# A four-stage macaron network on one core: the conditional tiles of the routed FFN moved ahead of the main experts, its table and zero writes moved to other places

## The chip, the cores and the metric

The kernel runs on one NeuronCore of a Trainium2 chip. The metric is the device time of one execution in microseconds (us). Before the change its median over 8 runs is 1976.63 us, from 1973.01 to 1981.93.

The core has five engines with instruction queues of their own, which meet through semaphores: PE (TensorE: matmuls; its weight loads are listed as PEld), DVE (VectorE), ACT (ScalarE), POOL (GpSimd) and SP (SyncE, which here only issues transfers). SP, ACT and POOL can each start DMA transfers from their queue. In the profile a name with a q behind it (PEq, POOLq, SPq) is the engine's sequencer: branches, semaphore steps and DMA issues.

## The reference

The activations are x of [2, 512, 256] in fp32: T = 1024 tokens of D = 256. Ten stages with residual additions follow each other: an FFN, an attention and an FFN of layer 0, one stage of layer 1, FFN, attention, FFN of layer 2, FFN, attention, FFN of layer 3 (the FFNs of one layer share their weights; each FFN's result is added with a factor 0.5). The FFNs of layers 0 and 3 are routed, and they are what the change touches. In the text they are FFN1 and FFN2 (layer 0), FFN3 and FFN4 (layer 3), in the order of time. Layer 0's reads:

```python
scores = softmax(x2d @ wg_router.T)                 # 32 experts
topk_w, topk_idx = top_k(scores, 6)
topk_w = topk_w / (sum(topk_w) + 1e-20)
C = 2 * (T * 6 // 32)                               # capacity of an expert: 384 slots
pos_in_e = position of the token in its expert's list
valid = pos_in_e < C                                # what does not fit is dropped
g = einsum('ecd,edf->ecf', xe, w_gate);  u = einsum('ecd,edf->ecf', xe, w_up)
ye = einsum('ecf,efd->ecd', silu(g) * u, w_down)    # F = 176
y = sum over the 6 of  y_tok * topk_w
out = y + silu(x2d @ ws_gate) * (x2d @ ws_up) @ ws_down   # shared expert, 352 wide
```

Layer 3's has 8 experts, 2 of them for a token, sigmoid scores, a factor 2.5, no capacity below T, and a shared expert of 176. The norm ahead of each FFN is a layer norm without weights.

## The kernel before, in words

`moe()` (L638) is called four times, by `l0_ffn` and `l3_ffn`. The 1024 tokens lie as 128 partitions by 8 chunks (P = 128, NC = 8), in two halves of four chunks (B = 2, CB = 4). The text of the program sets the order of instructions on each engine only in part: a scheduler places them, and two means tie it down. `in_order` (L141) chains all instructions of the named engines that are issued inside it, and leaves the last one of each in a dictionary `tail`. `issue_after(i)` keeps what stands inside it behind instruction i.

One routed FFN goes like this:

- Six gather buffers `xes` are cleared by POOL. The pool of weights has five buffers: the shared expert's `wsh` and four experts' `we` fill it, and the fifth expert takes the place of `wsh`.
- Front: per half, four warm-up matmuls, the layer norm (DVE takes moments at L215 and L216; POOL computes the reciprocal deviation `ln_rstd` in two steps, an addition at L224 and a power at L225; DVE writes `xn` at L230), then PE transposes `xn` (L184) into `xT`. The router's logits follow (L326). These are chained on PE and ACT. Behind them, ACT puts the two halves of `xn` into `table` in DRAM (L675), from which tokens are gathered later.
- Where the capacity is below T (FFN1 and FFN2), POOL's queue writes zeros over `rows` in DRAM, eight transfers of 768 KB (L681), so that dropped tokens contribute nothing.
- Scores: in FFN1 and FFN2 a softmax of DVE steps around one exp of ACT (L746 to L751). `topk` (L308 to L318), then `slot_lists` (L424 to L514): DVE builds the one-hot rows `sl_ol` and `sl_oh` (L465, L467, L476), PE multiplies them (`ps_sl`, L484), transposes (`ps_slt`, L504), and DVE writes the index lists `sl_put` and `sl_get` (L513, L514). The normalised scores `lg` go beside the rows in `table` (L692, from ACT's queue).
- The shared expert (`shared_unit`, L364): gate and up products (`pg`, `pu`, L376), silu on ACT (L379), the product `h` on DVE (L380), the down product `acc` on PE (L386), and x <- x + acc on DVE (L404).
- `experts_sparse` (L517) for the main tiles, the first two slot tiles of an expert in layer 0, three in layer 3: it loads an expert's three weights from SP's queue (L530 to L532), POOL gathers a tile of tokens with an indirect DMA (`xe`, L538), PE transposes it (`ps_xe`, L554, DVE copies it to `xeT`), multiplies with gate and up (`ps_gu`, L566), DVE and ACT make `he`, PE transposes it and multiplies with down (`ps_ye`, L591), and POOL scatters the result to `rows` (L596). Before the first tile PE runs eight warm-up passes (L164).
- `prepare_next` (L175) issues what the next stages want early: rows and columns of constants on POOL's queue (among them the bias row of layer 1's FFN, which DVE multiplies by 0.5 at L1113), and loads of layer 2's weights on SP's queue.
- Behind the experts stands a conditional: an integer `over`, computed with the lists, says whether any expert has more tokens than the main tiles hold. All engines load it (L706) and branch (L708); where it is not zero, `experts_sparse` runs once more for the remaining tiles. In the profiled execution the body is not executed: L538 ran 176 times, 128 for layer 0 and 48 for layer 3, which are the main tiles.
- `add_rows` (L714): SP loads a token's result rows back (`y<-rows`, L721) and they are added to x, by DVE (L731, L734) or through PE (`ps_add`, L727).

Of the kernel before, what the change touches and what calls it, by code (L numbers as in the profile page):

```python
# [15 lines left out]
PSUM = bass.MemoryType.PSUM  # L16
DRAM = bass.MemoryType.DRAM

P = 128
B, S, D = 2, 512, 256  # L20
T = B * S
NC = T // P
# [61 lines left out]
class Net:  # L84
# [554 lines left out]
    def moe(self, pre, names, E, F, K, FS, PER, tiles, cap, r, scores, scale):  # L639


        nc, tc, a = self.nc, self.tc, self.a
        router, wg, wu, wd, sg, su, sd = (a[pre + n] for n in names)
        RW = D + E
        self.calls += 1
        with ExitStack() as es:
            lists = es.enter_context(tc.tile_pool(name="f0li", bufs=1))
            table = self.dram.tile([T, RW], F32, name=f"table{self.calls}")
            rows = self.dram.tile([r * T, D], F32, name=f"rows{self.calls}")
            rv = rows.rearrange("(c p n) d -> c p n d", p=P, n=r)  # L650
            xes = [lists.tile([P, 2, RW], F32, name=f"xe{i}") for i in range(6)]
            for t in xes:
                nc.gpsimd.memset(t, 0.0)
            with ExitStack() as fs:
# [6 lines left out]
                with tc.tile_pool(name="ln", bufs=1) as lp:  # L661
                    tv = table[:, :D].rearrange("(b c p) d -> b p c d", p=P, b=B)
                    rT = self.router_weights(sb, psM, router, E)
                    tail, xns = {}, []
                    with self.in_order(tail, ("PE", "Activation")):
                        for b in range(B):
                            self.warm(psM, 4)
                            xn = lp.tile([P, CB, D], F32, name=f"xn{b}")
                            self.layernorm(lp, xn, b, *self.scales(lp, b))
                            xns.append(xn)  # L670
                            for k in range(KD):
                                self.transpose_tokens(xn, xT, psM, b, k)
                        s = self.logits(sb, psM, xT, rT, E, warm=True)
                        for b in range(B):
                            nc.scalar.dma_start(tv[b], xns[b])  # L675
                if cap < T:

                    zero = lists.tile([P, D], F32, name="zero")
                    nc.vector.memset(zero, 0.0)
                    for c in range(NC):  # L680
                        nc.gpsimd.dma_start(rv[c, :, :K, :], zero.unsqueeze(1).to_broadcast([P, K, D]))  # L681
                m = sb.tile([P, NC], F32, name="m")
                scores(s, m)
                mask = self.topk(sb, s, E, K)
# [4 lines left out]
                nc.vector.reciprocal(m, m)  # L689
                nc.vector.tensor_scalar(m, m, scale, None, ALU.mult)  # L690
                nc.vector.tensor_tensor(s, s, m.unsqueeze(2).to_broadcast([P, NC, E]), ALU.mult)
                nc.scalar.dma_start(table[:, D:].rearrange("(c p) e -> p c e", p=P), s)  # L692
                blocks = self.load_shared(sg, su, sd, FS)
                with tc.issue_after(tail["PE"]):
                    for half in range(B):
                        self.shared_unit(work, psA, psM, xT, blocks, half, 0.5)
                over = lists.tile([1, 1], I32, name="over")
                nc.vector.tensor_scalar(over, full[0:1, :], float(len(tiles) * P), None, ALU.is_gt)
            ew = es.enter_context(tc.tile_pool(name="f0e", bufs=1))
            with tc.tile_pool(name="f0p", bufs=1, space=PSUM) as psE:  # L700
                self.puts = []
                args = (table, rows, (get, put), (wg, wu, wd), list(range(E)), F)
                self.experts_sparse(ew, psE, xes, *args, tiles, PER)
            self.prepare_next()
            with tc.tile_pool(name="f0q", bufs=1, space=PSUM) as psE:
                some = nc.values_load(over[0:1, 0:1], min_val=0, max_val=1)  # L706
                wp = es.enter_context(tc.tile_pool(name="f0o", bufs=3))
                with tc.If(some > 0):  # L708
                    rest = list(range(len(tiles), -(-cap // P)))
                    self.experts_sparse(ew, psE, xes, *args, rest, PER, ahead=0, wp=wp)  # L710

        ys = {}

# [1494 lines left out]
```

## Time and profile before

| What | Value |
|---|---|
| Median of 8 runs | 1976.63 us (1973.01 to 1981.93) |
| The profiled execution | 1972.45 us, span 1970.6 us |
| Mean granted TensorE clock in it | 0.955 |
| PE / DVE / POOL / ACT busy | 90% / 58% / 46% / 41% of the span |
| DMA | 226.55 MB, 115 GB/s in the mean |
| first slice of the span (49 us) | PE 6 tenths, DMA 9 tenths, 318 GB/s |
| Queues: SP / POOL / ACT | 170.17 MB / 48.45 MB / 5.72 MB |
| FFN1, FFN2: zeros, 8 transfers | POOL's queue, landing 4.8 / 9.9 / 16.9 us after issue (min / median / max) |
| First expert product (`ps_gu`) in FFN1, 2, 3, 4 | 79.95, 503.25, 1170.17, 1888.43 us |
| First result rows loaded back (`y<-rows`) in FFN1, 2, 3, 4 | 248.75, 671.52, 1238.56, 1955.20 us |

The span is cut into 40 equal slices for the coarse view. In a timeline a line gives start, duration, engine, line of the program, operation, out<-in with shapes and count, and in brackets the idle time of the engine before it and what ended that. A group line gives an operation, how often, the shortest, median and longest duration in ns, and the first and last start in us.

### The profile page before, as it was taken

The numbers are of one execution on the slowest core, as the hardware profiler recorded it, in microseconds if no ns is written. First come the engines' busy times: TensorE is split into PE (matmuls) and PEld (weight loads), VectorE is DVE, ScalarE is ACT, GpSimd is POOL, SyncE is SP. The second block draws the span as 40 slices with busy tenths as digits, with TensorE's granted clock in tenths as the row PEclk, the third lists the DMA queues.
The fourth block names the chain that finished last, engine by engine and source line by source line (L and its number), as shares of the span: only waits on it lengthen the run. The fifth ranks groups of instructions, "written<-read, shape, count | busy, mean of one in ns | idle before, by whom it ended". The sixth has DMA issues, their size and how long they took to land. (4 is left out here: it accounts for less than half of the span.)

```text
span 1970.6 us, 30298 instructions
## 1 busy us (share of the span) xinstructions
PE 1768.1 (90%) x10848; PEld 1267.1 (64%) x10848; DVE 1151.5 (58%) x2771; ACT 804.8 (41%) x1380; POOL 911.4 (46%) x915
## 2 busy tenths in 40 slices
PE   6999859899999878899788999789999899999895
PEld 4677626465777655544465467567777677777674
DVE  4533366317433366655676653588777777777543
ACT  1133223311233124410662012377777687777221
POOL 3377746320777540110133126136657457666363
PEclk8999979899999888999899999899999999999998
DMA  9266450040566520000230023534454444544133
GB/s 318 76 192 187 158 193 12 1 160 27 159 188 187 188 91 1 1 22 0 98 109 23 0 60 96 163 129 128 157 170 150 146 154 152 170 150 141 45 100 98
DMA packets 117445, 226.55 MB, mean 115 GB/s; under 512 B 22382, under 2 KB 68828, under 8 KB 117014
## 3 DMA queue, kind: packets, MB, share of 16 engines
q1 hardware_dynamic: 88134, 170.17, 26.9%
q0 software_dynamic: 20608, 48.45, 7.9%
q10 hardware_dynamic: 8528, 5.72, 0.9%
q8 instruction: 96, 1.57, 0.3%
q14 instruction: 79, 0.65, 0.1%
HBM read 195.59 MB, written 41.81 MB: 120 GB/s over the span
## 5 line engine op out<-in xcount | busy, mean ns | idle before, releaser
L538 POOL DMA_INDIRECT xe<-table,sl_get x176 | 179.9, 1022 | 198.6 <-DVE sl_get L514 146.0
L566 PE MATMUL ps_gu<-we,xeT 128*128 128x352 f32 x704 | 224.6, 460 | 0.0
L596 POOL DMA_INDIRECT rows<-ye,sl_put x176 | 176.9, 1005 | 74.1 <-issue 39.6
L1759 DVE SCALAR_TENSOR_TENSOR xc<-pp,L_attn_cols,xc 128x511 f32<-128x511 f32 (+2 forms) x216 | 161.5, 748 | 30.8 <-ACT xc L1755 25.5
L591 PE MATMUL ps_ye<-we,hT 88*128 88x256 f32 x704 | 168.1, 379 | 2.9 <-ACT ye L132 1.7
L571 DVE SCALAR_TENSOR_TENSOR he<-se,xe,ps_gu 128x176 f32<-128x176 f32 x176 | 70.0, 398 | 167.4 <-ACT se L570 165.9
L566 PEld LDWEIGHTS ps_gu<-we,xeT 128*128 128x128 f32 x704 | 126.3, 190 | 55.4 <-DVE xeT L130 1.3
L591 PEld LDWEIGHTS ps_ye<-we,hT 88*128 88x128 f32 x704 | 133.1, 190 | 36.7 <-ACT ye L132 3.6
L1890 PE MATMUL pz<-xT,wt 128*128 128x128 f32 x1152 | 143.5, 278 | 12.3 <-ACT xt L1839 6.2
L1866 DVE SCALAR_TENSOR_TENSOR lm<-lm,jb,top 128x128 f32<-128x128 f32 x576 | 153.7, 342 | 0.0
L1890 PEld LDWEIGHTS pz<-xT,wt 128*128 128x128 f32 x1152 | 136.3, 193 | 17.7 <-issue 9.2
L1975 PE MATMUL yacc<-wt,y 128*128 128x256 f32 x576 | 143.5, 392 | 2.5 <-POOL y L1945 2.2
L1752 PE MATMUL pp<-xT,wx 128*128 128x512 f32 x288 | 139.3, 607 | 3.6 <-ACT dec L1743 0.9
L570 ACT ACTIVATE se<-ps_gu 128x176 f32<-128x176 f32 x176 | 55.9, 318 | 205.2 <-PE ps_gu L566 205.2
L1945 POOL TENSOR_TENSOR y<-y,sg 128x512 f32<-128x512 f32 x72 | 91.7, 1274 | 100.5 <-DVE y L1944 94.5
L1883 POOL TENSOR_TENSOR ce<-ce,CT 128x1024 f32<-128x1024 f32 x54 | 127.9, 2369 | 0.0
L1552 PE MATMUL ps_y<-w8T,xT 128*128 128x512 f32 x256 | 124.2, 619 | 0.0
L1975 PEld LDWEIGHTS yacc<-wt,y 128*128 128x128 f32 x576 | 104.2, 190 | 25.7 <-issue 10.4
L1918 PE MATMUL py<-lm,xt 128*64 128x128 f32 x1152 | 108.4, 282 | 12.1 <-ACT xc L1755 4.5
L1875 DVE TENSOR_TENSOR lm<-lm,M 128x1024 f32<-128x1024 f32 x72 | 87.2, 1216 | 48.4 <-ACT lm L1871 45.5
L1956 POOL TENSOR_TENSOR sqs<-sqs,sq 128x512 f32<-128x512 f32 x56 | 71.4, 1274 | 92.7 <-ACT sq L1955 92.7
L1906 POOL TENSOR_TENSOR xd<-xt,dec 128x512 f32<-128x512 f32 x54 | 56.3, 1043 | 94.7 <-ACT xt L1839 94.7
(404 smaller groups left out, 3528.5 us busy)
## 6 DMA issues: line engine op xcount, KB each, us to landing
lm<-rows SPq DMA_DIRECT2D x72, 512.0 KB
ce<-rows SPq DMA_DIRECT2D x54, 512.0 KB
rows<-zero POOLq DMA_DIRECT2D x16, 768.0 KB, 9.9
y<-rows SPq DMA_DIRECT2D x16, 768.0 KB
we<-in_L_ffn_w_gate_dram SPq DMA_DIRECT2D x64, 176.0 KB
we<-in_L_ffn_w_up_dram SPq DMA_DIRECT2D x64, 176.0 KB
we<-in_L_ffn_w_down_dram SPq DMA_DIRECT2D x64, 176.0 KB
we<-in_L_ffn_w_dram SPq DMA_DIRECT2D x48, 176.0 KB
```

The costliest lines, as they stand in the source:

```text
L538: nc.gpsimd.indirect_dma_start(xe[:, i, :], None, table, bass.IndirectOffsetOnAxis(get[:, e * per + j : e * per + j + 1], 0), bounds_check ...
L566: nc.tensor.matmul(pg, xeT[:, k, i * P : (i + 1) * P], wgu[:, :, k], start=(k == 0), stop=(k == KD - 1))
L591: nc.tensor.matmul(py[:, i, :], hT[:, q, i * P : (i + 1) * P], wd[:, q, :], start=(q == 0), stop=(q == 1))
L596: put_rows = nc.gpsimd.indirect_dma_start(rows, bass.IndirectOffsetOnAxis(put[:, e * per + j : e * per + j + 1], 0), y[:, i, :], None, bou ...
L1552: nc.tensor.matmul(ps, xT[:, k, :], self.w8T[:, k, 2 * e2 : 2 * e2 + 2, :], start=(k == 0), stop=(k == KD - 1))
L1752: nc.tensor.matmul(pp, wv[:, k, :], xT[:, k, b * S : (b + 1) * S], start=(k == 0), stop=(k == KD - 1))
L1759: nc.vector.scalar_tensor_tensor(out[:, 3 - w :], pp[:, : S - 3 + w], cw[:, m, w : w + 1], out[:, 3 - w :], ALU.mult, ALU.add)
L1866: nc.vector.scalar_tensor_tensor(k["lm"][:, h, :], k["lm"][:, h, :], jb[:, k["c"], n : n + 1], top, ALU.add, ALU.min)
L1883: nc.gpsimd.tensor_tensor(k["ce"], k["ce"], ct, ALU.mult)
L1890: nc.tensor.matmul(pz[:, m, :], u["wz"][:, kk, m * P : (m + 1) * P], xT[:, kk, c * P : (c + 1) * P], start=(kk == 0), stop=(kk == KD - 1),)
L1918: nc.tensor.matmul(py[i * HP : (i + 1) * HP, m, :], w[:, h * HP : (h + 1) * HP], v[:, h, :], start=(m == 0 and n == 0), stop=(n == len(src ...
L1975: nc.tensor.matmul(yacc[cc // 2][:, cc % 2, :], k["y"][:, m, :], u["wo"][:, m, :], start=(u["g"] == 0 and m == 0 and cc % 2 == 0), stop=(u ...
```

## The change

Six things move; what is computed stays, apart from six memsets in the body of the conditional.

1. The shared expert's weights are requested ahead of the norm in the text.
2. Each half of `xn` goes to the table from SP's queue as soon as it is written, not from ACT's queue behind the logits. The normalised scores go to the table from SP's queue as well.
3. POOL's instructions are chained in the front too, and the zero rows stand behind the last of them, the second half's power.
4. The conditional tiles stand ahead of the main experts, so all engines load `over` and branch between the shared expert and the first expert. The body clears the six gather buffers first.
5. The main experts' loads stand behind the put of the second half of `xn`.
6. `prepare_next` stands behind that put and behind POOL's last step of the front.

```diff
                     rT = self.router_weights(sb, psM, router, E)
-                    tail, xns = {}, []
-                    with self.in_order(tail, ("PE", "Activation")):
+                    blocks = self.load_shared(sg, su, sd, FS)
+                    tail = {}
+                    with self.in_order(tail, ("PE", "Activation", "Pool")):
                         for b in range(B):
                             self.warm(psM, 4)
                             xn = lp.tile([P, CB, D], F32, name=f"xn{b}")
                             self.layernorm(lp, xn, b, *self.scales(lp, b))
-                            xns.append(xn)
+                            put_x = nc.sync.dma_start(tv[b], xn)
                             for k in range(KD):
                                 self.transpose_tokens(xn, xT, psM, b, k)
                         s = self.logits(sb, psM, xT, rT, E, warm=True)
-                        for b in range(B):
-                            nc.scalar.dma_start(tv[b], xns[b])
                 if cap < T:

                     zero = lists.tile([P, D], F32, name="zero")
                     nc.vector.memset(zero, 0.0)
-                    for c in range(NC):
-                        nc.gpsimd.dma_start(rv[c, :, :K, :], zero.unsqueeze(1).to_broadcast([P, K, D]))
+                    with tc.issue_after(tail["Pool"]):
+                        for c in range(NC):
+                            nc.gpsimd.dma_start(rv[c, :, :K, :], zero.unsqueeze(1).to_broadcast([P, K, D]))
...
-                nc.scalar.dma_start(table[:, D:].rearrange("(c p) e -> p c e", p=P), s)
-                blocks = self.load_shared(sg, su, sd, FS)
+                nc.sync.dma_start(table[:, D:].rearrange("(c p) e -> p c e", p=P), s)
                 with tc.issue_after(tail["PE"]):
                     for half in range(B):
                         self.shared_unit(work, psA, psM, xT, blocks, half, 0.5)
...
             ew = es.enter_context(tc.tile_pool(name="f0e", bufs=1))
-            with tc.tile_pool(name="f0p", bufs=1, space=PSUM) as psE:
-                self.puts = []
-                args = (table, rows, (get, put), (wg, wu, wd), list(range(E)), F)
-                self.experts_sparse(ew, psE, xes, *args, tiles, PER)
-            self.prepare_next()
-            with tc.tile_pool(name="f0q", bufs=1, space=PSUM) as psE:
+            self.puts = []
+            args = (table, rows, (get, put), (wg, wu, wd), list(range(E)), F)
+
+            with tc.tile_pool(name="f0q", bufs=1, space=PSUM) as psE, tc.tile_pool(name="f0o", bufs=3) as wp:
                 some = nc.values_load(over[0:1, 0:1], min_val=0, max_val=1)
-                wp = es.enter_context(tc.tile_pool(name="f0o", bufs=3))
                 with tc.If(some > 0):
+
+                    for t in xes:
+                        nc.gpsimd.memset(t, 0.0)
                     rest = list(range(len(tiles), -(-cap // P)))
                     self.experts_sparse(ew, psE, xes, *args, rest, PER, ahead=0, wp=wp)
+            with tc.tile_pool(name="f0p", bufs=1, space=PSUM) as psE:
+                with tc.issue_after(put_x.ins):
+                    self.experts_sparse(ew, psE, xes, *args, tiles, PER)
+            with tc.issue_after(put_x.ins), tc.issue_after(tail["Pool"]):
+                self.prepare_next()
```

In the order of instructions that the scheduler makes of it, PE's list changes only where the experts start (load of `over`, branch, then all eight warm-up passes ahead of the first `ps_xe`; before, four of them stood behind it). ACT loses its three transfers per FFN. The rows and columns of layer 1's constants move on POOL's queue from FFN1 into FFN2, behind the zeros there, and DVE's L1113 moves with them, from between L316 and L317 of FFN1 to behind the first step of L455 in FFN2. The expert loads on SP's queue come behind the table puts in all four FFNs.

## The prediction

> **What bounds the kernel now.** I read the page's engine shares first, then the timelines of ACT, DVE and POOL at the front of the first FFN, then the four places where the experts start and end, since these are what the diff touches.
>
> ```profile
> PE 1768.1 (90%) x10848; PEld 1267.1 (64%) x10848; DVE 1151.5 (58%) x2771; ACT 804.8 (41%) x1380; POOL 911.4 (46%) x915
> ```
>
> TensorE is the bound as an average, so this change, which takes no matmul away, can only pay where PE waits. The slices show such places in each FFN's front, above all in the first 49 us (6 tenths). The ACT timeline there:
>
> ```profile
> 32.44 2.45 ACTq L675 DMA_DIRECT2D table<-xn  x2
> 34.93 0.42 ACT L748 ACTIVATE lg<-lg 128x256 f32<-128x256 f32 x1 [12.14 <-DMA we<-in_L_ffn_w_down_dram]
> ```
>
> ACT puts the normed rows into the table ahead of the softmax's exp; the first put could issue only at 32.4, with the DMA engines full. DVE in the same stretch:
>
> ```profile
> 15.68 2.22 DVE L230 TENSOR_SCALAR xn<-x,ln_mv,ln_rstd 128x256 f32<-128x256 f32 x6 [2.24 <-POOL ln_rstd L225]
> ...
> 29.63 0.42 DVE L747 TENSOR_TENSOR lg<-lg,m 128x256 f32<-128x256 f32 x1
> 35.38 0.42 DVE L749 TENSOR_REDUCE m<-lg 128x8 f32<-128x256 f32 x1 [5.33 <-ACT lg L748]
> ...
> 42.31 0.29 DVE L1113 TENSOR_SCALAR row_L_ffn_bias<-row_L_ffn_bias 128x256 f32<-128x256 f32 x1 [1.89 <-DMA row_L_ffn_bias<-in_L_ffn_bias_dram]
> ```
>
> Three stalls lie in the chain that ends in the slot lists: the norm waits for POOL, the sum for ACT's exp, and a bias row of layer 1, which has no hurry, holds the queue. POOL shows why the first is late, and how long the zero writes take; first FFN1, then FFN2:
>
> ```profile
> 12.22 0.23 POOL L224 TENSOR_SCALAR ln_rstd<-ln_mv 128x4 f32<-128x4 f32 x1 [6.46 <-DVE ln_mv L216]
> 13.52 0.23 POOL L224 TENSOR_SCALAR ln_rstd<-ln_mv 128x4 f32<-128x4 f32 x1 [1.08 <-DVE ln_mv L216]
> 13.69 0.87 POOL L681 DMA_DIRECT2D rows<-zero  x1
> 14.58 2.20 POOL L225 TENSOR_TENSOR ln_rstd<-ln_rstd,mhalf 128x4 f32<-128x4 f32 x2
> ```
>
> ```profile
> 404.03 6.77 POOL L681 DMA_DIRECT2D rows<-zero  x8
> ...
> 447.29 1.04 POOL L225 TENSOR_TENSOR ln_rstd<-ln_rstd,mhalf 128x4 f32<-128x4 f32 x1
> ```
>
> In FFN2 the zeros already went out during the attention, 40 us ahead of the norm. The start of the experts in FFN1 and, in the group of the conditional's line, what a branch costs each engine:
>
> ```profile
> 76.95 1.10 PE L164 MATMUL warm<-cst 128*128 128x256 f32 x4 [0.87 <-DVE x L404]
> ...
> 79.01 1.03 PE L164 MATMUL warm<-cst 128*128 128x256 f32 x4
> ...
> 79.95 2.63 PE L566 MATMUL ps_gu<-we,xeT 128*128 128x352 f32 x8
> ```
>
> ```profile
> L708 DVEq COMPARE_BRANCH  x4: 62/63/72, 239.2 to 1948.6; - x4
> ...
> L708 PEldq COMPARE_BRANCH  x4: 3357/3432/3602, 240.0 to 1949.2; - x4
> ...
> L708 POOLq INC_SWDGE_SEM  x4: 362/1418/1896, 246.8 to 1953.9; - x4
> ```
>
> The columns are min/median/max ns. The branch takes 3.4 us on PE's weight-load sequencer, under 0.1 us elsewhere. At the end of the experts in FFN2 it stands ahead of the adds:
>
> ```profile
> 669.95 2.47 PE L164 MATMUL warm<-cst 128*128 128x256 f32 x5 [4.03 <-DVEq L708]
> 671.52 0.81 SPq L721 DMA_DIRECT2D y<-rows  x2
> ```
>
> **Part 1, the front of FFN1.** The zeros move behind both pow steps. The first pow can follow its L224 at once: 12.53 to 13.57 against 14.58 to 15.62, so xn begins near 13.6 instead of 15.68: 2.0 us. The exp loses ACT's puts ahead of it: DVE L747 ended at 30.05, now 28.05, exp 0.42, L749 at 28.55 instead of 35.38: 6.8 us earlier. The bias row's wait and its operation (1.89 + 0.29) leave this FFN: the chain is then 9.0 us ahead at L317. DVE is busy without a gap from there to the one-hot rows, so ps_sl (64.51) and the last slot list (sl_get, 73.33) follow; the shared unit's first product h, bound by PE's pu, comes 8.9 earlier. I take **+8.9**. What covers the moved puts: SP issues them ahead of 12 expert loads and the tables, but everything landed by 51 and the first gather then goes at 64.9, so 14 us are left. Should the puts and zeros cost all of that and more, the gain is bounded below by 0, above by 9.0.
>
> **Part 2, zeros and layer 1's constants in FFN2.** Before, eight zero writes took 20 us to land (405.4 to 425.3), beside attention. Now they issue from 448.3 (end of the last pow) and land by 471 to 473 with the table writes beside them; the constants that follow on POOL's queue wait for them, and the bias row lands near 474. It now sits on DVE's queue behind sl_vi, which DVE reaches at 471.7. Queued behind it are the one-hot rows, 13.65 us of them, for which PE waited 3.09 at 487.04. Price: wait 2.3, operation 0.29, and an x<-acc add of 0.6 that moves ahead of the rows: **-3.2**. Bounds: 0.9 if the row lands in time; 9 if the row, issued near 465 when the first zeros have landed, takes the 14.7 us to landing that it took in FFN1 (479.7, a wait of 8). In FFN2 to FFN4 ACT's own puts (0.93 us at 450.67) delayed nothing; taking them away is worth 0, since exp waits for DVE.
>
> **Part 3, the branch at the start of the experts, four times.** It is now behind the shared unit's last products and ahead of the warm matmuls. PE's sequencer runs ahead of the array by up to 16 weight loads (the branch at 240.0 in FFN1 ran while products of 239.33 to 241.30 did), and 18 products of 4.15 us (14 of 3.29 in FFN4) stand in front: the 3.4 us are mostly covered. DVE reaches its branch only after the x add that already gates the warm matmuls, and its semaphore comes 0.5 us later. All eight warm passes (2.14 us together) now come before the first transposed rows, where four came between. First product near 80.95 instead of 79.95: **-1.0 each, -4.0**. The experts' phases are PE's (5.0 us a unit), so the delay is not won back. Bounds: -0.5, and -3.7 with DVE's late code as at 666.5, where its branch ended and its semaphore came only at 669.8. -4.5 if PE's branch is uncovered (3.4) and the array restarts slow (1.1, from the warm matmuls below). SP, POOL and ACT take the branch too: POOL was idle 33 us before its first gather, SP's next load is for the fifth expert, needed 20 us later, ACT's first expert work comes 1.5 us behind PE: nothing.
>
> On the restart: after the 4.03 us idle at 669.95 in FFN2, 36 warm matmuls took 10.97 us, 305 ns each; after 3.53 us idle in FFN3, 38 took 10.46, 275 each. The longer idle thus cost some 1.1 us more (36 x 30 ns). [...]
>
> **Part 4, the end of the experts.** There the branch goes and with it what POOL does behind it. FFN1: last scatter ends 244.47, POOL's semaphore step starts at 246.8 and lasts 1.90, y<-rows starts 248.75; now it can start 1.9 earlier: **+1.9**. FFN2: step 1.52 from 670.0, plus the restart of 36 warm matmuls: **+2.2** (1.75 to 3.1). FFN3: step 0.36, **+0.7**. FFN4: 1.31 from 1953.9, y at 1955.20, **+1.6**. If the last scatter's landing alone holds y (in FFN4 the chain shows 3.80 us of it), the ends still give the steps' own time, 5.1 together; 0 if the semaphore steps stay.
>
> **Sum.** FFN1 8.9 - 1.0 + 1.9 = 9.8; FFN2 -3.2 - 1.0 + 2.2 = -2.0; FFN3 -0.3; FFN4 +0.6: 8.1 us. The profiled execution took 1972.45 (span 1970.6, 1.9 around it), 4.2 below the median of 1976.63. Against the median: **1968.5 us**.
>
> **Rivals.**
> - Late code on DVE at all four starts: for it 666.5 to 669.8, against it the other three branches with 0.5. 4 x 2.7 more = 10.8, so 1979.3: within 0.2%.
> - The bias row 9 us late in FFN2: gain 2.3, 1974.3, within 0.2%. For it FFN1's 5.12 us waits of POOL's queue on zeros; against it 326 GB/s of zeros alone.
> - FFN1's 8.9 does not come, because the puts on SP land late behind x and the shared weights, or exp then waits for something else: -0.8, so 1977.4, same.
> - The other side: PE's branch is not covered at the starts. PE then idles 3.4 us behind the x add and restarts slow: 4.5 each, 14.0 more, 1982.5, slower by 0.3%. It decides from 4.0 us a start. For it: at the ends, PE's wait was 4.03 and 3.53; against it: there only 8 products stood ahead, at the starts 14 to 18.
>
> **How the numbers follow.** Measurement tells 0.2%, 4 us. Chances: forecast (gain 4 to 13, 1963.5 to 1972.6) 0.64; late code on DVE 0.08; late bias 0.08; FFN1's gain lost 0.07; PE's branch uncovered or a code wait on another engine, slower, 0.13. Inside the likeliest case the low end takes FFN2 at -0.9 and starts at -0.5 (2.3 + 2.0 more): 1964; with FFN2's end at its bound 1963. The high end takes in the rivals within 0.2% but not the slower one: 1978.5. Faster 0.65, same 0.21, slower 0.14.
>
> **What would show it.** Right: in FFN1 ACT's exp at 28 and L749 at 28.5 without a 5 us wait; sl_get near 64.4; no DMA on ACT's queue in these FFNs; in FFN2 a DVE wait of 1 to 4 us before the bias row; first gu 8 us earlier in FFN1 and 4 later in FFN2, relative to their fronts; y<-rows within 3.5 us of the last scatter's end. Wrong: PE idle of 3 us or more before the warm matmuls, zeros still landing when the first scatter wants to go, or a gather that waits for a table put.

## The result, and the profile after

The changed kernel takes 1996.28 us (median of 16 runs, 1982.05 to 1998.79) against 1976.61 of the kernel before: the ratio is 1.0082, with a 95% interval from 1.0069 to 1.0096. It is slower by 0.8%, where 0.4% faster was forecast. The profiled execution took 1990.57 us (span 1988.7), 5.7 below its median; its span is 18.1 above that of the kernel before. The time follows the granted clock of TensorE from execution to execution: in the changed kernel the fastest (1982.05) has a mean of 0.952, the slowest (1998.79) one of 0.944. A second set on another occasion gave 1.0088 (1.0065 to 1.0111):

> The changed kernel once more, beside the kernel before on the same chip, as the line for the other three. All theories: slower than before; 0.8% where the experts' phases last 156 us from first to last gate/up product of FFN1, less where they last 190 and are not TensorE's.

The engine shares on the page hardly moved. TensorE is busy for 16.0 us more with the same 10848 matmuls, so it did not only wait: it ran slower in places.

```profile
PE 1784.1 (90%) x10848; PEld 1275.3 (64%) x10848; DVE 1149.9 (58%) x2771; ACT 804.9 (40%) x1380; POOL 912.9 (46%) x915
```

To see where the 18.1 us are, I cut both traces at the same instructions: the norm's first output (`xn` L230; in FFN3 that of the second half, as the first half is done 34 us earlier), the end of the list `sl_get` (L514), the first and the last gate/up product (`ps_gu` L566), the end of the last scatter (L596), and the first load of result rows (`y<-rows`). All in us, before -> after:

| Stretch | FFN1 | FFN2 | FFN3 | FFN4 | Sum of the changes |
|---|---|---|---|---|---|
| Front: to the end of sl_get (FFN1 from 0, others from xn) | 73.5 -> 62.9 | 52.7 -> 63.1 | 31.9 -> 31.9 | 35.7 -> 35.7 | -10.6, +10.4 |
| Start: sl_get to the first ps_gu | 6.4 -> 13.6 | 6.6 -> 13.0 | 6.5 -> 10.4 | 6.5 -> 11.3 | +22.2 |
| First to last ps_gu | 155.9 -> 157.7 | 155.9 -> 159.1 | 57.2 -> 58.9 | 57.2 -> 59.5 | +8.9 |
| Last ps_gu to the last scatter's end | 8.6 -> 8.6 | 8.6 -> 8.6 | 8.5 -> 6.7 | 6.7 -> 6.6 | -1.8 |
| End: last scatter to y<-rows | 4.3 -> 1.5 | 3.8 -> 2.8 | 2.7 -> 1.2 | 2.9 -> 1.1 | -7.0 |
| From y<-rows to the next xn (or the end) | 195.2 -> 194.1 | 460.3 -> 455.2 | 607.6 -> 608.8 | 15.4 -> 16.4 | -4.0 |

The front of FFN1 and the ends gained what was forecast. The four starts lost 22 us, and behind them the products took 9 more, at a granted clock of 0.63, 0.50, 0.66 and 0.53 (76.4 to 81, 514 to 519, 1182 to 1187 and 1905 to 1910 us; in the kernel before it is 1.00 behind all four starts). FFN2's front lost 10.4, where 3.2 were forecast. What the starts lost in waiting is about what FFN1's front, the ends and the two small rows gained (22.2 against 23.4); the rest, 10.4 and 8.9, go nearly all with TensorE at a lower clock (in FFN2's front 0.51 from 445 to 460 us). The mean granted clock is 0.948 over 1988.7 us, and was 0.955 over 1970.6. The share of the clock that was withheld, times the span, is 103 us against 89: an estimate from these numbers is that up to 15 of the 18.1 us are work at the lower clock.

VectorE's timeline of the changed kernel at the front of FFN1 shows the first gain:

```profile
12.85 2.44 DVE L230 TENSOR_SCALAR xn<-x,ln_mv,ln_rstd 128x256 f32<-128x256 f32 x6 [0.17 <-POOL ln_rstd L225]
...
26.49 0.42 DVE L753 TENSOR_REDUCE m<-lg 128x8 f32<-128x256 f32 x1 [0.48 <-ACT lg L752]
```

The norm waits 0.17 us for POOL, the sum 0.48 for exp; both waits of 2.24 and 5.33 are gone. Now the start of FFN1's experts, from the timeline of all engines:

```profile
62.69 0.22 DVE L514 TENSOR_SCALAR sl_get<-sl_put 128x128 int32<-128x128 int32 x1
...
69.96 3.83 PE L164 MATMUL warm<-cst 128*128 128x256 f32 x8 [4.53 <-DVEq L704]
70.75 1.10 POOL L538 DMA_INDIRECT xe<-table,sl_get  x1 [41.11 <-DVEq L704]
...
76.48 4.33 PE L566 MATMUL ps_gu<-we,xeT 128*128 128x352 f32 x8 [0.84 <-DVE xeT L130]
```

The kernel before had at this place:

```profile
73.84 1.12 POOL L538 DMA_INDIRECT xe<-table,sl_get  x1 [33.12 <-DVE sl_get L514]
```

The list is ready at 62.91, but POOL issues the first gather at 70.75, 7.84 us later; before, it was 0.29 (list at 73.55). The brackets name the cause: gather and warm-up both waited for VectorE's sequencer at line 704, the conditional. The eight first products then take 4.33 us where they took 2.63; that 1.7 is what FFN1's stretch from the first to the last product has grown by. The group of that line, with min/median/max in ns:

```profile
L704 PEldq COMPARE_BRANCH  x4: 3356/3694/3770, 63.4 to 1893.2; - x4
L704 DVEq COMPARE_BRANCH  x4: 56/63/67, 66.1 to 1896.6; - x4
...
L704 DVEq EVENT_SEMAPHORE  x4: 21/21/21, 69.8 to 1897.2; - x4
...
  POOL xe L538: 158.7, 4
  PE warm L164: 10.8, 4
```

TensorE's branch in FFN1 ran from 63.4 to 66.8, under shared products that ended at 65.4: it was mostly covered, as the prediction had it. VectorE reached its own branch at 66.1, behind the last x addition, and its next step came only at 69.8. All four first gathers and all four warm-ups waited for the conditional; each of the four gathers starts 0.90 to 0.93 us behind VectorE's step there. Not everything behind the conditional waits so: SP issued the last part of an expert's weights at 68.74, before VectorE's step.

```profile
68.74 0.36 SPq L532 DMA_DIRECT2D we<-in_L_ffn_w_down_dram  x1
```

### The profile page after: what moved, and what is told of

It reads as the page before. It is cut to its first block, busy times and chain, and to the rows that moved or that the text cites. A ratio compares the mean times of both kernels' runs of the same rounds, so it can differ in the third digit from the quotient of the medians.

```text
span 1988.7 us, 30364 instructions
## 1 busy us (share of the span) xinstructions
PE 1784.1 (90%) x10848; PEld 1275.3 (64%) x10848; DVE 1149.9 (58%) x2771; ACT 804.9 (40%) x1380; POOL 912.9 (46%) x915
## 5 line engine op out<-in xcount | busy, mean ns | idle before, releaser
L566 PE MATMUL ps_gu<-we,xeT 128*128 128x352 f32 x704 | 232.7, 473 | 3.4 <-DVE xeT L130 3.4
L596 POOL DMA_INDIRECT rows<-ye,sl_put x176 | 177.0, 1006 | 78.9 <-issue 39.0
L566 PEld LDWEIGHTS ps_gu<-we,xeT 128*128 128x128 f32 x704 | 130.1, 196 | 62.1 <-issue 5.9
L1894 PE MATMUL pz<-xT,wt 128*128 128x128 f32 x1152 | 142.9, 277 | 12.4 <-ACT xt L1843 6.3
L164 PE MATMUL warm<-cst 128*128 128x256 f32 x282 | 88.9, 454 | 12.9 <-DVEq L704 10.8
```

Source lines behind the costliest of these rows:

```text
L566: nc.tensor.matmul(pg, xeT[:, k, i * P : (i + 1) * P], wgu[:, :, k], start=(k == 0), stop=(k == KD - 1))
L596: put_rows = nc.gpsimd.indirect_dma_start(rows, bass.IndirectOffsetOnAxis(put[:, e * per + j : e * per + j + 1], 0), y[:, i, :], None, bou ...
L1894: nc.tensor.matmul(pz[:, m, :], u["wz"][:, kk, m * P : (m + 1) * P], xT[:, kk, c * P : (c + 1) * P], start=(kk == 0), stop=(kk == KD - 1),)
```

## The experiments

Theory S, formed from this trace: the place of the conditional does it, since the gathers and the warm-up behind it wait until VectorE has passed. Rival F: the fronts do it, zeros and constants behind the norm. The first four kernels ran on another chip, on which the kernel before takes 2076.07 us; the experts' phase of FFN1 is 190 us there instead of 156, so only ratios and the stretches around it can be compared. In the changes shown, a line in parentheses stands in words for several.

**The conditional back behind the experts.**

```diff
+            (main experts, prepare_next)
             with tc.tile_pool(name="f0q", ...) as psE:
                 some = nc.values_load(over[0:1, 0:1], min_val=0, max_val=1)
                 with tc.If(some > 0):
-                    for t in xes:
-                        nc.gpsimd.memset(t, 0.0)
                     self.experts_sparse(ew, psE, xes, *args, rest, PER, ahead=0, wp=wp)
-            (main experts, prepare_next)
```

> The changed kernel with one part undone: the conditional tiles stand behind the main experts again, as before; table puts, zero rows and constants stay as changed. Theory S (the starts of the experts): the conditional in front costs 5 to 10 us at each of the four starts, 29 us together in the trace of the changed kernel, and saves some 8 at the ends; without it about 1970 us (FFN2's front still some 3 to 9 us late), and the first gather follows sl_get by 0.3 us in all four FFNs. Rival F (the fronts: zeros and constants behind the norm): the loss stays, 1990 us or more.

Measured: ratio to before 0.9955 (0.9931 to 0.9979), faster. The four stretches from sl_get to the first product are 6.4, 6.6, 6.4 and 6.5 us again, the gather follows the list by 0.28 or 0.29; in FFN1:

```profile
63.06 1.10 POOL L538 DMA_INDIRECT xe<-table,sl_get  x1 [33.08 <-DVE sl_get L514]
```

Theory S holds, F falls. FFN2's lists are late, and for the reason the prediction gave, as VectorE's timeline there shows:

```profile
498.35 0.29 DVE L1114 TENSOR_SCALAR row_L_ffn_bias<-row_L_ffn_bias 128x256 f32<-128x256 f32 x1 [3.50 <-DMA row_L_ffn_bias<-in_L_ffn_bias_dram]
```

**The conditional alone, in the kernel before.**

```diff
+            (load of over, tc.If with memsets and the remaining tiles, in pools f0q and f0o)
             (main experts, prepare_next)
-            (load of over, tc.If with the remaining tiles)
```

> The kernel before with that one part alone: the conditional tiles stand in front of the main experts (with the six memsets in the body), all else as before. Theory S: about 1976.6 + 29 - 8 = 1997 us, first gather 4 to 8 us behind sl_get, first gate/up product 7 to 10 us behind the last x<-x+acc instead of 3. Rival F: 1974 to 1979 us.

Measured: ratio 1.0042 (1.0019 to 1.0064), slower by 8 us instead of 20. The starts are as expected: 13.6, 13.2, 12.2 and 11.1 us from list to first product, 24 us more than before, the ends 6.8 us shorter. The direction is shown, the size was missed on this chip: there the experts' phases of FFN1 and FFN2 (190.3 and 192.1 us here, 191.4 and 188.4 with the conditional behind) do not follow the start as they do where they take 156. What limits them there was not looked into, and the conditional alone was not run on a chip of the other kind.

**FFN2's zero rows ahead of the norm again.**

```diff
-                    with tc.issue_after(tail["Pool"]):
+                    with tc.issue_after(tail["Pool"]) if self.calls == 1 else ExitStack():
                         for c in range(NC):
```

> The changed kernel with the zero rows of FFN2 alone where they were, ahead of the norm (written during the attention); FFN1's stay behind the norm, layer 1's constants stay in FFN2, the conditional stays in front. If the 9 us that FFN2's front lost in the trace of the changed kernel come from the zeros beside the norm: 1987 us. If they come from the conditional or from the clock of TensorE alone: within 2 us of the changed kernel, 1994 to 1998.

Measured: ratio 1.0001 (0.9980 to 1.0022) on that chip, where the changed kernel itself was not run, so the time decides nothing. In the trace the stretch from the logits to sl_get is 40.05 us, against 43.27 in the changed kernel and 39.53 before. These 3.2 us are mostly not the price of the zeros, though. VectorE's timeline of the changed kernel in that stretch, with two waits for TensorE's products and, between them, the bias row, for which it does not wait:

```profile
463.95 0.69 DVE L380 SCALAR_TENSOR_TENSOR h<-s,pu 128x512 f32<-128x512 f32 x1 [1.97 <-PE pu L376]
...
474.90 0.28 DVE L1117 TENSOR_SCALAR row_L_ffn_bias<-row_L_ffn_bias 128x256 f32<-128x256 f32 x1
...
497.84 0.35 DVE L497 TENSOR_SCALAR sl_ld<-ps_sl,cst 128x128 f32<-128x128 f32 x1 [5.58 <-PE ps_sl L484]
```

and the same two waits in this kernel:

```profile
498.00 0.69 DVE L380 SCALAR_TENSOR_TENSOR h<-s,pu 128x512 f32<-128x512 f32 x1 [0.70 <-PE pu L376]
...
529.96 0.35 DVE L497 TENSOR_SCALAR sl_ld<-ps_sl,cst 128x128 f32<-128x128 f32 x1 [3.96 <-PE ps_sl L484]
```

The two waits differ by 1.27 and 1.62 us, nearly the whole 3.2: it is TensorE that was later. The 6.6 us between norm and logits stayed (18.88 against 19.80, before 13.17); the zeros are gone from there, so they are not the cause. What zeros and constants cost in the lists is seen where TensorE's clock was nearly full, as with the conditional back behind the experts (a wait of 3.50 us, with 9 tenths of the clock or more in that slice of the page).

**A body of only the six memsets**, conditional in front.

```diff
                 with tc.If(some > 0):
                     for t in xes:
                         nc.gpsimd.memset(t, 0.0)
-                    rest = list(range(len(tiles), -(-cap // P)))
-                    self.experts_sparse(ew, psE, xes, *args, rest, PER, ahead=0, wp=wp)
```

> The changed kernel with the conditional in the same place but a body of only the six memsets; the remaining slot tiles are left out (none are run with this data). It tells the code that is jumped over apart from the conditional's meeting of the engines. If the length of the jump makes the starts late (3.4 us on TensorE's sequencer, 3 us on VectorE's): TensorE's branch falls below 0.5 us, the starts are 3 to 4 us shorter each, 1981 to 1985 us. If the meeting itself costs it (the gather waits until all engines have passed): branch short, but the gather still 4 us behind sl_get, 1990 us or more.

Measured: ratio 0.9917 (0.9894 to 0.9941). From list to first product 8.0, 7.9, 9.0 and 8.2 us. The group of the conditional's line, and POOL's timeline:

```profile
L704 PEldq COMPARE_BRANCH  x4: 207/215/228, 47.7 to 1956.3; - x4
```

```profile
63.80 1.10 POOL L538 DMA_INDIRECT xe<-table,sl_get  x1 [33.46 <-DVE sl_get L514]
```

The branch is short, and the gather again waits for the list, not for VectorE's conditional. But two things left at once, the long jump and the body's use of PE, ACT and DVE. The next kernel separates them.

**One expert in the body**, conditional in front: a short body that uses all engines. It and the two around it ran on a chip where the kernel before takes 1976.55 us.

```diff
-                    self.experts_sparse(ew, psE, xes, *args, rest, PER, ahead=0, wp=wp)
+                    self.experts_sparse(ew, psE, xes, *args[:4], [0], F, rest, PER, ahead=0, wp=wp)
```

> The changed kernel with the conditional in front and in its body one expert's remaining tiles instead of all experts': the other experts' remaining tiles are left out (none run with this data). [...] If the meeting makes the gather late: it starts behind VectorE's last step of the conditional, 4 us behind sl_get, in all four FFNs, and TensorE's branch is below 0.5 us: some 5 us a start later than before less 2.5 for the short code, about 6 us faster than the changed kernel. If the length of the code does all of it: as with the body of six memsets, gather 0.8 us behind sl_get, 12 us or more faster than the changed kernel.

Measured: 1986.87 us, ratio 1.0052 (1.0033 to 1.0071), 8 us faster than the changed kernel beside it (1994.90), and 10 slower than before. The 8 us do not price the short code: 7.3 of the 7.8 us between the two profiled spans lie in FFN2's front, where TensorE ran slow in the changed kernel's trace and not in this one (from 447 to 497 us the page gives the clock as 7 tenths there and 9 here). The stretches do: the four starts sum to 43.8 us, against 50.5 in the changed kernel beside it and 48.3 in its first profile.

```profile
L704 PEldq COMPARE_BRANCH  x4: 219/330/625, 63.5 to 1893.5; - x4
...
L704 DVEq EVENT_SEMAPHORE  x4: 21/21/21, 66.4 to 1897.2; - x4
...
  POOL xe L538: 107.5, 3
  PE warm L164: 3.9, 4
```

In FFN1 VectorE's step now comes at 66.4, 0.2 us behind its branch instead of 3.7, so that part went with the length of the code, in FFN1 and FFN2. The gathers are nevertheless 4.39, 4.22, 4.20 and 4.13 us behind sl_get, and 0.89 to 0.93 behind VectorE's step: that is the meeting. It holds the gather back until VectorE's last x addition (3.25 us behind the list) and the branch are over, and so it takes away the time in which the gather ran beside the shared unit's end. TensorE's branch, too, took 3.4 to 3.8 us over the whole body and 0.2 to 0.6 over the short one; why the long jump takes longer was not shown. The meeting is the larger part.

How far the meeting reaches is not shown. The main experts' gathers fill the buffers that the body fills as well, and TensorE and VectorE read them there. A wait for these two readers would look the same as a wait for all engines, and SP's load, which shares no buffer with the body, was not held. A body with gather buffers of its own was not run.

**Warm-up passes ahead of the conditional.**

```diff
                         self.shared_unit(work, psA, psM, xT, blocks, half, 0.5)
+                last = next(i for i in reversed(nc.cur_bb.bb.instructions) if i.engine.name == "PE")
+                with tc.issue_after(last):
+                    self.warm(psM, 8)
```

> The changed kernel with eight more warm-up instructions (16 passes, 4.3 us) on TensorE ahead of the conditional, behind the shared unit, in all four FFNs. TensorE then idles little while the conditional is passed. If a slow clock after that idle time costs the 1.7 to 3.2 us a phase by which the experts' first-to-last product time grew in the changed kernel: those go back to 155.9 and 57.2, and the kernel is 6 to 9 us faster than the changed one, 1986 to 1989. If the clock is not the cause, or the passes themselves delay the first product: 1994 to 1998.

Measured: 1991.72 us, ratio 1.0081 (1.0059 to 1.0103): no gain against the changed kernel (1.0082). TensorE's timeline at FFN1's start:

```profile
64.64 3.62 PE L164 MATMUL warm<-cst 128*128 128x256 f32 x16
69.07 2.29 PE L164 MATMUL warm<-cst 128*128 128x256 f32 x8 [0.82 <-DVEq L707]
73.00 0.36 PE L554 MATMUL ps_xe<-cst,xe 128*128 128x128 f32 x1 [1.64 <-DMA xe<-table,sl_get]
74.00 0.62 PE L554 MATMUL ps_xe<-cst,xe 128*128 128x128 f32 x3 [0.64 <-DMA xe<-table,sl_get]
75.47 5.06 PE L566 MATMUL ps_gu<-we,xeT 128*128 128x352 f32 x8 [0.84 <-DVE xeT L130]
```

The wait for the conditional shrinks to 0.82, but the late gather leaves gaps behind the warm-up, and the first products run slow all the same (5.06 us for eight; first to last ps_gu 158.8 us, 2.9 above before). So they are no faster where the wait for the conditional is 0.82 us than where it is 4.53 (4.33 us for the eight). The passes also cost something. In FFN3 TensorE reaches its branch only behind them, at 1172.09, so that all of it (to 1175.81) lies behind the shared products. The next warm-up waits for it, and the gather starts 0.8 us behind it:

```profile
1176.12 2.29 PE L164 MATMUL warm<-cst 128*128 128x256 f32 x8 [0.72 <-PEq L707]
```

The gathers of FFN3 and FFN4 are 7.2 and 6.8 us behind the list instead of 4.6 and 4.4, and the four starts sum to 54.9 us instead of 48.3. The time is no longer for it, but in this trace FFN2's front has no slow stretch between norm and logits, which is worth some 6 us.

**The conditional behind and FFN2's zeros ahead**, all else as changed (the edits of the first and third kernel together).

> The changed kernel with the conditional behind the main experts again and with FFN2's zero rows ahead of the norm again; FFN1's front stays as changed. Theory S with the zeros' price: 10.6 us gained in FFN1's front stay, FFN2 loses at most 0.5: 10 us faster than before, 0.5%, and 3 us faster than with the conditional alone put back. If the gain of FFN1's front is lost later on: within 2 us of before.

Measured: 1958.04 us, ratio 0.9903 (0.9887 to 0.9919), 18.5 us faster than the kernel before in the medians and 12.4 in the two profiled spans. It beats both kernels. In its trace TensorE has no slow stretch in FFN2's front either. FFN1's sl_get ends at 62.4, FFN2's stretch from logits to list is 39.12, all starts are 6.4 to 6.5 us.

**What made FFN1's gain.** The forecast laid 6.8 us to ACT's puts. In the version just shown I put them back on ACT:

```diff
-                            put_x = nc.sync.dma_start(tv[b], xn)
+                            xns.append(xn)
...
                         s = self.logits(sb, psM, xT, rT, E, warm=True)
+                        for b in range(B):
+                            put_x = nc.scalar.dma_start(tv[b], xns[b])
...
-                nc.sync.dma_start(table[:, D:]...
+                nc.scalar.dma_start(table[:, D:]...
```

> As the version with the conditional behind and FFN2's zeros ahead, but with the table's rows and scores put from ACT's queue again, behind the logits. It prices this part of FFN1's front: by the prediction exp comes at 32 to 35 us instead of 26, and the kernel is 6 to 7 us slower than that version. Rival: the puts were late before only because the zeros and the bias row stood around them; then exp is at most 2 us later and the time within 2 us of that version.

Measured: 1961.13 us, ratio 0.9921 (0.9908 to 0.9935): the gain stays. ACT's timeline at FFN1's front shows why:

```profile
17.76 1.42 ACTq L676 DMA_DIRECT2D table<-xn  x2
25.58 0.42 ACT L751 ACTIVATE lg<-lg 128x256 f32<-128x256 f32 x1 [7.30 <-DVE lg L750]
```

The puts go out at 17.8, not at 32.4. So it was not the queue as such. Next, FFN1's zeros ahead of the norm, first with the puts on SP, then with the puts on ACT:

```diff
-                    with tc.issue_after(tail["Pool"]) if self.calls == 1 else ExitStack():
+                    with ExitStack():
                         for c in range(NC):
```

> The version with the conditional behind and FFN2's zeros ahead (1958 us), now with FFN1's zero rows too where they were, between POOL's norm steps. By the prediction's step the norm's second input comes 2 us later: 1960. Rival: the zeros' traffic also delays the puts and loads that the scores wait for, and most of the 10.6 us goes: 1966 or more.

> As the version with the table put from ACT's queue (1961 us), with FFN1's zero rows ahead of the norm as well. There ACT's puts went out at 17.8 us and held nothing; in the kernel before they went out at 32.4. Theory Z: it is the zeros standing ahead, and the order that this gives the transfers, that held ACT's puts: exp comes at 32 to 35 us again and the kernel is 6 us slower than that version, 1967. Rival: the zeros cost their 1.5 us in the norm and no more, exp at 27 to 28, 1962.

With SP's puts 1956.98 us, ratio 0.9909 (0.9890 to 0.9928): the zeros ahead cost nothing that the time shows, and 1.6 us in the trace (sl_get at 64.0). With ACT's puts 1971.65 us, ratio 0.9978 (0.9967 to 0.9990), sl_get at 74.8, and ACT stands as in the kernel before:

```profile
32.57 2.42 ACTq L676 DMA_DIRECT2D table<-xn  x2
35.04 0.42 ACT L751 ACTIVATE lg<-lg 128x256 f32<-128x256 f32 x1 [13.88 <-DMA we<-in_L_ffn_w_down_dram]
```

So either edit frees exp: the puts on SP, or the zeros behind the norm. Only with both undone do ACT's puts wait for an expert's weight loads. Last, the two remaining parts alone in the kernel before: the puts on SP, and layer 1's constants moved to FFN2.

```diff
-                            xns.append(xn)
+                            nc.sync.dma_start(tv[b], xn)
...
-                        for b in range(B):
-                            nc.scalar.dma_start(tv[b], xns[b])
...
-                nc.scalar.dma_start(table[:, D:].rearrange("(c p) e -> p c e", p=P), s)
+                nc.sync.dma_start(table[:, D:].rearrange("(c p) e -> p c e", p=P), s)
```

```diff
-                    with self.in_order(tail, ("PE", "Activation")):
+                    with self.in_order(tail, ("PE", "Activation", "Pool")):
...
-            self.prepare_next()
+            with tc.issue_after(tail["Pool"]):
+                self.prepare_next()
```

> The kernel before with the table's rows and scores put from SP's queue alone; zeros, constants, loads and conditional as before. By the prediction's step exp is freed: it comes at 30 us, and since the bias row still holds VectorE behind it, 5 to 7 us of FFN1's front are gained: 1970 us. If the bias row or the zeros hold it then: within 2 us of before.

> The kernel before with POOL's chain and layer 1's constants moved into FFN2 alone; puts, zeros and conditional as before. By the prediction 2.2 us (the bias row's wait and operation) are gained in FFN1 and at most 1 lost in FFN2: 1975. If fewer transfers in FFN1's front also free ACT's puts, up to 9 us: 1968.

The puts alone give 1.0011 (0.9998 to 1.0024), the constants alone 0.9980 (0.9964 to 0.9996), against 1975.53 us. Exp comes at 30.27 with the first, and then the bias row holds VectorE; with the second the bias row is gone, and exp is later than before:

```profile
41.92 0.29 DVE L1111 TENSOR_SCALAR row_L_ffn_bias<-row_L_ffn_bias 128x256 f32<-128x256 f32 x1 [6.16 <-DMA row_L_ffn_bias<-in_L_ffn_bias_dram]
```

```profile
34.76 1.91 ACTq L675 DMA_DIRECT2D table<-xn  x2
36.71 0.42 ACT L749 ACTIVATE lg<-lg 128x256 f32<-128x256 f32 x1 [16.48 <-DMA we<-in_L_ffn_w_down_dram]
```

sl_get then ends at 74.9 and 75.0 us in FFN1, no earlier than before (73.5); with both, as in the kernel with the zeros ahead and the puts on SP (which has the moved loads too), at 64.0. Each wait covers the other. The times say less than the traces here: the profile of the puts alone is that of its slowest execution (1985.19) and has TensorE's slow stretch in FFN2's front, and what gives the constants alone their 0.2% does not lie in FFN1's front.

**The conditional's price behind the experts.** In the fastest version, once without any conditional and once with one expert in its body:

```diff
-                with tc.If(some > 0):
-                    rest = list(range(len(tiles), -(-cap // P)))
-                    self.experts_sparse(ew, psE, xes, *args, rest, PER, ahead=0, wp=wp)
```

```diff
-                    self.experts_sparse(ew, psE, xes, *args, rest, PER, ahead=0, wp=wp)
+                    self.experts_sparse(ew, psE, xes, *args[:4], [0], F, rest, PER, ahead=0, wp=wp)
```

> The same version (conditional behind) without any conditional: the remaining slot tiles are left out (none run with this data). It prices the conditional behind the experts: y<-rows follows the last scatter by 1.5 us instead of 2.4 to 4.1, 8 us together, 1950 us. If the scatter's landing sets y and not the conditional: within 2 us of 1958.

> The same version (conditional behind) with one expert's remaining tiles in the body instead of all: the others' are left out (none run with this data). If the jump's length is what the conditional costs behind the experts: as without a conditional, 1950 us. If the meeting of the engines and POOL's wait for its outstanding scatters cost it: 1956 to 1959.

Measured: 1954.38 us, ratio 0.9902 (0.9884 to 0.9921), and 1954.63 us, 0.9905 (0.9877 to 0.9934), beside a before of 1974.97. The traces show the ends shorter without the conditional (1.49, 1.49, 1.18 and 1.13 us from scatter to y, instead of 4.10, 3.92, 2.35 and 3.10), but against 0.9903 with the whole conditional the ratios cannot tell a gain. Behind the experts it costs a few us at most.

## Why the prediction was wrong

Against the forecast of 8.1 us gained, the profiled spans show 18.1 lost. In these 26.2 the starts are 18.2 worse than forecast, the slow products behind them 8.9 and FFN2's front 7.2; FFN1's front, the ends and the two small rows of the table are 8.1 better. The failed step is the price of the branch at the starts; had it held, the rest would have given a gain of 9.0.

- **FFN1's front, +8.9:** right in size (10.6 measured), and the three waits it named did go. The share of each was wrong. The 6.8 us were put down to ACT's puts in the queue, as if the terms could be added; the puts alone gave nothing, since the bias row then waited 6.16 us. The size held because the change undid all of them at once.
- **Zeros and constants in FFN2, -3.2:** right only where TensorE's clock was nearly full there (9 tenths or more in that slice of the page in the two runs named next). The bias row waited 2.80 us (one expert in the body) and 3.50 (conditional behind) against the forecast 2.3, and the lists came 3.1 and 3.9 us later than before. With the zeros ahead that is gone. In the changed kernel itself the row was not waited for, since VectorE came late to it; the 10.4 us that this front lost go nearly all with TensorE's clock (below), for which the sum had no term.
- **The branch at the start, -1.0 each:** this is the step that failed. Measured in the mean: 5.6 us each in waiting (22.2 together) and 2.2 each in slow products (8.9). The bounds of -0.5 and -4.5 were wrong too. The false sentence is that POOL "was idle 33 us before its first gather", so that the branch there costs nothing. POOL did pass the conditional long before, at 39 us in FFN1. But the gather behind it started only 0.90 to 0.93 us behind VectorE's step, which comes behind the x addition, and with the warm-up ahead, in FFN3, 0.8 us behind TensorE's branch. I moved the gathers from beside the shared unit's end to behind it without counting that, though they are instructions queued behind the moved step. Even with short code the gathers stay 4.1 to 4.4 us behind the list, where they were 0.3.
- **The rivals:** what the prediction calls late code on VectorE came in two of the four starts (its step comes 3.7 and 2.9 us behind its branch in FFN1 and FFN2, 0.5 to 0.6 in the other two); that it is code that comes late was my reading; the runs show 0.2 us with the short body in FFN1. This case was priced within 0.2% because it left the gather where it was. TensorE's uncovered branch, the slower case at 1982.5, did not come true in the profiled execution, where the branch ended at 1175.10 and 1896.92 in FFN3 and FFN4, within 0.1 us of the x addition: the place was right, the mechanism was another. The cover is not sure: in the second set's profile that branch took 4.37 us in FFN4, and warm-up and gather waited for it. The measured time lies 14 us above this case too.
- **The clock:** the sum has no term for products at a low clock behind the starts; the prediction priced a slow restart (1.1 us) only for an uncovered branch. TensorE was in fact idle for 4.53 us in FFN1 and 3.66 in FFN2, and the eight products behind that took 4.33 and 5.06 us (clock 0.63 and 0.50). In FFN3 and FFN4 no single gap was that long, and they took 4.33 and 4.93 us all the same (clock 0.66 and 0.53). So what sets the low clock off behind the starts was not shown. FFN3, then FFN4:

```profile
1175.76 3.87 PE L164 MATMUL warm<-cst 128*128 128x256 f32 x8 [1.37 <-DVEq L704]
...
1182.35 4.33 PE L566 MATMUL ps_gu<-we,xeT 128*128 128x352 f32 x8 [0.84 <-DVE xeT L130]
```

```profile
1901.22 0.36 PE L554 MATMUL ps_xe<-cst,xe 128*128 128x128 f32 x1 [1.59 <-DMA xe<-table,sl_get]
1903.26 0.92 PE L554 MATMUL ps_xe<-cst,xe 128*128 128x128 f32 x3 [1.67 <-DMA xe<-table,sl_get]
1905.01 4.93 PE L566 MATMUL ps_gu<-we,xeT 128*128 128x352 f32 x8 [0.84 <-DVE xeT L130]
```

What I missed beside it is 6.6 us between the norm and the logits of FFN2, and most of the 3.7 behind them. The windows of the changed kernel there, and then of the kernel before (busy time of PE, PEld, DVE, ACT and POOL, then the clock, DMA share and GB/s):

```profile
445.00:450.00 5.00, 5.00 (x23) 4.55 (x22) 0.69 (x1) 1.87 (x2) 5.00 (x7) 0.54 0.99 304
450.00:455.00 5.00, 5.00 (x19) 4.55 (x18) 0.00 (x0) 0.00 (x0) 1.11 (x3) 0.50 1.01 330
455.00:460.00 5.00, 5.00 (x15) 3.61 (x14) 1.29 (x4) 0.45 (x2) 0.61 (x2) 0.50 1.02 383
490.00:495.00 5.00, 3.80 (x144) 3.80 (x148) 2.25 (x5) 0.61 (x1) 0.00 (x0) 0.50 0.02 5
```

```profile
450.00:455.00 5.00, 5.00 (x38) 4.74 (x37) 0.69 (x1) 1.87 (x2) 0.00 (x0) 1.00 0.60 210
```

From 445 to 460 TensorE is busy all the time, at half clock, so this is no wait. The kernel with the puts alone on SP, which has neither zeros nor a conditional at this place, shows it too, with little DMA traffic:

```profile
455.00:460.00 5.00, 5.00 (x19) 4.53 (x18) 0.00 (x0) 0.00 (x0) 0.00 (x0) 0.50 0.00 0
```

The kernel with one expert in the body, which has the zeros and the conditional of the change, does not (its norm to logits is 13.15 us). So the slow clock at FFN2's front belongs to no part of the change that these runs name. Both profiles of the changed kernel have it; each of the others was profiled in one execution only, and the clock differs between executions of one kernel (means of 0.943 to 0.953 in the changed kernel). What sets it off there stays open, and so does how much of the 0.8% it makes.
- **The ends, +6.4:** right in sum, 7.0 measured (FFN2's 1.0 against 2.2, the other three more than forecast). But the time of the version without a conditional shows that such a stretch need not come back whole.

## What to carry to other kernels

Here the four first gathers behind a conditional waited for VectorE to pass it, though it was skipped, and started 4.4 to 7.8 us behind their list instead of 0.3: list what stands behind a conditional and had so far run ahead, above all gathers that hide their latency there, and put the conditional where nothing runs ahead. When several waits stand in one chain, do not add what each is worth: undo them singly and together, as one can take the place of the other (here the bias row's 6.16 us that of the wait for exp). The late starts cost twice here, 22.2 us in waiting and 8.9 in products at a granted clock of 0.50 to 0.66. And a profile is one execution: where the granted clock differs between two of them, first sum what lies at the lower clock, before a stretch is put down to an edit.

## What the runs showed of the hardware

- A skipped conditional took 3.4 to 3.8 us on TensorE's sequencer in the changed kernel's trace when the code jumped over was long (3.4 to 3.6 in the kernel before, 4.37 once in the second set's profile), 0.2 us with six memsets and 0.2 to 0.6 with one expert. On VectorE the branch itself took 0.06 us, but the next step came 3.7 and 2.9 us later in FFN1 and FFN2, and 0.5 to 0.6 us later in FFN3 and FFN4.
- Behind sixteen warm-up passes, eight more and gaps of 0.82, 1.64, 0.64 and 0.84 us (3.9 together), eight products took 5.06 us that took 2.63 in the kernel before.
- TensorE ran at half clock for 10 us and more in FFN2's front (granted 0.54, 0.50 and 0.50 from 445 to 460 us) while it was busy 5.00 us of 5.00, in some of these traces and not in others with the same instructions there.
- Two puts on ACT's queue kept ACT idle for 12 to 16 us ahead of exp (12.14, 13.88 and 16.48), until weight loads that SP had issued were in, and with the puts in the same place they went out at 17.8 us instead of 32.6 when only POOL's zero writes stood elsewhere.
